# Layer 0's last image takes its norm, gate and projection band by band between its scans; layer 1's weights get another address

## The chip, the cores and the metric

The kernel runs on one core of a Trainium2 chip. A core has five engines that work side by side, each with its own instruction queue, executed in order: PE (TensorE, matrix products), DVE (VectorE), ACT (ScalarE), POOL (GpSimd) and SP, which here only issues transfers (DMAs). An instruction may wait on semaphores for work of other engines or for a transfer to land; everything queued behind it on its engine then waits too. The metric is device microseconds (us) of one execution; several runs are made and their median is given. Lines of the form L256 are line numbers of the kernel before.

## What is computed

The program is a stack of four layers on an input of 4 images, each 64x64 pixels of 128 channels; each layer adds its result to its input. The change lies in layer 0 and, for an address, in layer 1. Layer 0 is a two-dimensional selective scan (state space model) with 256 inner channels and 16 states:

```python
xz = x @ in_proj_w.T                      # x is group-normalized
xh, z = jnp.split(xz, 2, axis=-1)
z = silu(z)
xc = silu(depthwise_conv3x3(xh) + conv_b)
xs = stack([x0, x1, x0[..., ::-1], x1[..., ::-1]], axis=1)   # rows, columns, and both reversed
...
dA = jnp.exp(dt[..., None] * A)
h = dA * h + (dt * ut)[..., None] * bt[:, :, None, :]
y = jnp.einsum('bkdn,bkn->bkd', h, ct)
...
y = ys[:, 0] + ys[:, 2, :, ::-1]          # the four directions are added up (columns transposed)
...
mu = y.mean(-1, keepdims=True)
var = y.var(-1, keepdims=True)
y = (y - mu) / jnp.sqrt(var + EPS) * out_norm_w + out_norm_b
y = y * z
return y @ out_proj_w.T
```

The last five lines, per pixel over the 256 channels, are what the change moves for the last image: the norm, the gate `y * z` and the projection. Layers 1 (Fourier filters and a feed-forward part), 2 (a Fourier attention) and 3 (neighbourhood attention) follow.

## The kernel before

**Units and slots.** Layer 0 (`layer0`) works on one image after another. An image has 4096 pixels, cut into 8 bands (`NCH`) of 512 (`CH`). The scan of one band in one of the four directions is a *unit*: 32 units per image, 128 in all, directions in the order k = 1, 3, 0, 2, eight bands each. Directions 2 and 3 go through the bands backwards, so in the last eight units of an image (k = 2) band 7 comes first and band 0 last. Within a unit there are 16 *slots*, one per state (`NS`). A slot has one POOL product `dB` (L476), two ACT exponentials `dA` into PSUM (L482, three buffers), two DVE scans (L483), and a step of `transposed()`: PE transposes a piece of the states `h` of seven slots ago (`LAG`), ACT copies it out as `hT` (L380), PE multiplies it with C into `yT` (L405). At the unit's end DVE adds `yT` to `y` (L421); for k = 2, when all four directions are in, it also takes statistics of `y` (`bn_stats`, L424), and SP stores `y` to the scratch tensor `y2` (L426). Because of the lag this falls on slot 7 of the next unit; behind the very last scan the lag is worked off alone (`while queue or copied`).

**Order.** `manual_schedule` makes PE, ACT, DVE and POOL execute in the order in which the program calls them. SP's order is left to the framework's scheduler.

**Side work.** What is not a scan goes in between as generators, `before(b + 1)` (norm, gate and convolution inputs of the next image) and `after(b)` (what follows the scans of image b). A generator yields a letter for what its next piece needs: "l" loads, "f" is free to go anywhere, "m" needs the spare PSUM bank and so does not go into slots 6 to 10 (`BUSY`). A `Side` object paces it: `count` pieces over `slots` slots from slot `first`; a piece is due when its share of the time has passed. `later(place, ...)` puts a single instruction into a place of a coming slot.

**after(b).** First the statistics of all 32 pixel groups: 32 `bn_aggr` on DVE (L242) in four pieces, one square root on ACT and one reciprocal on DVE (`Shared.rstd`, L46 and L47), and a load of the table set for exponential and logarithm (`exp_and_ln`, L121), since the square root stands in another set. Then for each band: SP loads `yf` (from `y2`, L249) and `zf` (L251); DVE normalizes four 128x256 pieces (L256, two per "f" piece); PE transposes them into `pg` (L264) and ACT copies them out as `yg` with scale and bias (shown under L437, the line of the caller); POOL multiplies `yg` with the gate (L270) while SP loads the input `xr` (L269); PE projects (`op`, L275); DVE adds `xr` (L281, in `residual`) and SP stores the result to `x1` (L282). `after(b)` runs among the scans of image b + 1. For the last image there is no next one: `d.finish` runs it to its end behind the last scan.

**Layer 1 and 2.** Pools of SBUF memory are stacked in the order in which they are opened; a pool that is opened later takes the addresses of pools closed before. `layer1` opens its weights' pool `l1w` first, then its work pools, then loads the weights (`layer1_weights`, L581 on SP, L583 to L593 on ACT) and runs `layer1_image` four times: `load_image` (L701) and, at the end of each band, a store to `x2` (L696). Layer 2 then loads its own weights (L723).

Of the kernel before, what the change touches and what calls it, by code (L numbers as in the profile page):

```python
# [10 lines left out]
F32 = mybir.dt.float32  # L11
AF = mybir.ActivationFunctionType
ALU = mybir.AluOpType
AX = mybir.AxisListType
PSUM = bass.MemoryType.PSUM

P = 128
Q = 68
NB = 4
NT = 4096  # L20
DM = 128
NJ = NT // P
CH = 512
NCH = NT // CH
K4 = 4
WD = 32 * 129 * 16
NS = 16


class Shared:  # L30


    def __init__(self, tc, pool, A):
        nc = tc.nc
        self.nc, self.tc = nc, tc
        self.ident = pool.tile([P, P], F32, name="ident")
        make_identity(nc, self.ident)
        self.gmat = pool.tile([P, P], F32, name="gmat")
        nc.sync.dma_start(self.gmat, A["c_gmat"])
        self.eps5 = pool.tile([P, 1], F32, name="eps5")  # L40
        nc.vector.memset(self.eps5, 1e-5)
# [41 lines left out]
def layer0(sh, A, x_in, x_out, scr):  # L83
# [6 lines left out]
    tc, nc = sh.tc, sh.nc  # L90
    with ExitStack() as ctx:
        pool = lambda name, bufs, **kw: ctx.enter_context(tc.tile_pool(name=name, bufs=bufs, **kw))
        wp = pool("l0w", 1)
        tmp = pool("l0tmp", 2)
        small = pool("l0small", 2)
# [25 lines left out]
        exp_and_ln = lambda: nc.scalar.preload_act_table_set("natural_log_exp_and_others")  # L121
# [111 lines left out]
            nc.scalar.copy(xw, xo.rearrange("p (h w) -> p w h", w=64))  # L233
            nc.sync.dma_start(dst.rearrange("p (w h) -> p w h", h=64)[:, :, 8 * c : 8 * c + 8], xw)

        def after(b, st, later):

            mv = small.tile([P, NJ, 2], F32, name="ln_mv")
            for j in range(NJ):
                if j % 8 == 0:  # L240
                    yield "f"
                nc.vector.bn_aggr(mv[:, j, :], st[:, j])  # L242
            rs = sh.rstd(small, mv[:, :, 1], [P, NJ], "ln_r")
            exp_and_ln()
            for c in range(NCH):
                yield "l"
                rows = slice(c * CH, (c + 1) * CH)
                y = tmp.tile([P, 4, 2 * P], F32, name="yf", tag="t4", bufs=4)
                nc.sync.dma_start(y, tiles(scr(f"y2{b % 2}")[rows, :]))  # L249
                z = tmp.tile([P, 2, CH], F32, name="zf", tag="t4", bufs=4)  # L250
                nc.sync.dma_start(z, scr(f"z{b % 3}")[:, :, rows].rearrange("s p t -> p s t"))  # L251
                for q in range(4):
                    if q % 2 == 0:
                        yield "f"
                    j = 4 * c + q
                    nc.vector.tensor_scalar(  # L256
                        y[:, q, :], y[:, q, :], mv[:, j, 0:1], rs[:, j : j + 1], ALU.subtract, ALU.mult
                    )
                yg = tmp.tile([P, 2, CH], F32, name="yg", bufs=1)
                for s in range(2):  # L260
                    yield "m"
                    pt = spare("pg")
                    for q in range(4):
                        nc.tensor.transpose(pt[:, q * P : (q + 1) * P], y[:, q, s * P : (s + 1) * P], sh.ident)  # L264
                    norm = dict(scale=on_w[:, s : s + 1], bias=on_b[:, s : s + 1])
                    later("act0", nc.scalar.activation, yg[:, s, :], pt, AF.Identity, **norm)
                yield "f"
                xr = tmp.tile([P, 4, DM], F32, name="xr", tag="t2", bufs=4)
                nc.sync.dma_start(xr, tiles(x_in(b)[rows, :]))  # L269
                nc.gpsimd.tensor_tensor(yg, yg, z, ALU.mult)  # L270
                yield "m"
                op = spare("op").rearrange("p (q d) -> p q d", q=4)
                for q in range(4):
                    for s in range(2):
                        nc.tensor.matmul(  # L275
                            op[:, q, :], lhsT=yg[:, s, q * P : (q + 1) * P], rhs=w_out[:, s, :], start=(s == 0), stop=(s == 1)
                        )
                later("dve", residual, b, rows, xr, op)
# [65 lines left out]
        per = len(units) // NB  # L344
# [84 lines left out]
        sides = []  # L429
# [3 lines left out]
        slot = 0  # L433

        def later(place, f, *a, slots=1, **kw):

            todo.setdefault((slot + slots, place), []).append(lambda: f(*a, **kw))  # L437
# [10 lines left out]
        with tc.manual_schedule(engines=order):  # L448
            for i, (b, k, c) in enumerate(units):
                if i % per == 0:  # L450
                    ln_st = small.tile([P, NJ, 1, 6], F32, name="ln_st")
# [12 lines left out]
                for n in range(NS):  # L464
                    slot = NS * i + n
                    g, q = divmod(n, 4)
# [46 lines left out]
                    if n == 10:  # L513
                        y = unit["y"] = tmp.tile([P, 4, 2 * P], F32, name="y", tag="t4", bufs=4)
# [19 lines left out]
                    sides = [d for d in sides if d.need]  # L534
                if i + 1 < len(units):
                    u, bd, Wd = u_next, bd_next, Wd_next
                if i % per == per - 1:
                    slot += 1
                    for d in sides:
                        d.finish(flush_all)  # L540
                    sides = [Side(after(b, ln_st, later), 4 + 8 * 7, NS * (i + 1) + 8, 28 * NS)]
            while queue or copied:
                transposed()()
            for d in sides:
# [3 lines left out]
class Side:  # L548


    def __init__(self, pieces, count, first, slots):
        self.pieces, self.count, self.first, self.slots = pieces, count, first, slots
        self.done, self.run, self.free_at = 0, 0, first
        self.need = next(pieces)

# [3 lines left out]
        return self.need == "c" and self.run % 9 > 0  # L559

    def due(self, slot):
        return slot >= self.free_at and self.done * self.slots <= (slot - self.first) * self.count

    def step(self):
        self.done += 1
        self.run = self.run + 1 if self.need == "c" else 0
        self.need = next(self.pieces, None)
# [138 lines left out]
def layer1(sh, A, x_in, x_out):  # L706
    tc, nc = sh.tc, sh.nc
    with ExitStack() as ctx:
        pool = lambda name, bufs, **kw: ctx.enter_context(tc.tile_pool(name=name, bufs=bufs, **kw))
        wp = pool("l1w", 1)  # L710
        pools = pool("l1big", 2), pool("l1tmp", 2), pool("l1small", 2), pool("l1ps", 4, space=PSUM)
        w = layer1_weights(sh, A, wp)
        for b in range(NB):
            layer1_image(sh, w, pools, x_in(b), x_out(b))
# [1069 lines left out]
```

## Time and profile before

| What | us |
|---|---|
| median of 5 runs (8636.91 to 8653.36) | 8638.89 |
| the profiled execution, its own time | 8637.81 |
| its span, first to last instruction | 8636.0 |
| scans of image 0 (from 251.6) | 1456.1 |
| scans of image 1 | 1509.1 |
| scans of image 2 | 1509.0 |
| scans of image 3 (to 6132.8) | 1407.0 |
| behind the last scan, to the last residual of layer 0 | 115.1 |
| first load of layer 1's weights issued at | 6250.26 |
| first loads of layer 2 issued at | 6838.70 |

In the profile lines below, a group reads: line, engine, operation, output <- inputs, shapes, count | busy us, mean ns of one | idle us of the engine just before them, and what ended most of it. In an order of time a line reads: start us, duration us, engine, line, operation, tiles, shapes, count, and in brackets the engine's idle time before it and what released it. SPq and ACTq lines are the issue of a transfer, not its duration.

### The profile page before, as it was taken

To read this page: it belongs to the slowest core of one execution; us is meant where nothing else is said; L and a number is where in the kernel's file an instruction comes from. 1 tells how busy PE (TensorE), PEld (TensorE's weight loads), DVE (VectorE), ACT (ScalarE), POOL (GpSimd) and SP (SyncE) were. 2 spreads that over 40 slices of the span, in tenths; PEclk is the share of its full clock that TensorE was granted. 3 is DMA by queue.
4 is the path that set the end of the run, shared out by engine and by line. 5 is a ranking of instruction groups with operands and counts; after the bars stand their busy time and mean duration, and the time that the engine had idled before them with its cause. 6 is when DMAs were issued, how large, how long until landed. Compare 5 with 4: busy or idle time off the path is not lost. (4 is left out here: it accounts for less than half of the span.)

```text
span 8636.0 us, 140834 instructions
## 1 busy us (share of the span) xinstructions
PE 6675.1 (77%) x52976; PEld 4226.7 (49%) x52976; DVE 6815.9 (79%) x7900; ACT 6419.1 (74%) x10524; POOL 5539.1 (64%) x2518
## 2 busy tenths in 40 slices
PE   7688888777788777778877777777589677677689
PEld 3344454444445444444544444444377565464456
DVE  2689999998999999899999999999545533544578
ACT  6799999988888898888889989899422114416467
POOL 0689889988888898888889989999400010110233
PEclk9799999999999999999999999999789888788699
DMA  6345555445555454555545444445331231240332
GB/s 110 134 154 171 170 167 168 163 154 162 167 158 180 157 170 152 163 167 159 180 156 173 150 162 169 163 168 175 117 74 38 55 103 55 83 138 25 89 94 79
DMA packets 1292220, 1181.63 MB, mean 137 GB/s; under 512 B 640022, under 2 KB 1077874, under 8 KB 1224595
## 3 DMA queue, kind: packets, MB, share of 16 engines
q1 hardware_dynamic: 1289858, 1170.90, 43.4%
q8 instruction: 417, 6.83, 0.3%
q14 instruction: 265, 2.16, 0.1%
q10 hardware_dynamic: 1680, 1.74, 0.1%
HBM read 980.48 MB, written 189.74 MB: 136 GB/s over the span
## 5 line engine op out<-in xcount | busy, mean ns | idle before, releaser
L476 POOL TENSOR_TENSOR dB<-du,Bb 128x1024 f32<-128x1024 f32 x2048 | 4820.4, 2385 | 672.2 <-DVE h L483 496.6
L483 DVE TENSOR_TENSOR_SCAN h<-dA,state,dB 128x512 f32<-128x512 f32 x4096 | 4956.2, 1270 | 368.2 <-ACT dA L482 268.3
L370 PE MATMUL pt<-ident,h 128*128 128x128 f32 x16384 | 2267.1, 283 | 1070.6 <-ACT hT L380 1064.3
L482 ACT ACTIVATE dA<-delta,A_neg 128x512 f32<-128x512 f32 x4096 | 2748.1, 691 | 208.9 <-DVE h L483 185.9
L370 PEld LDWEIGHTS pt<-ident,h 128*128 128x128 f32 x16384 | 1853.7, 143 | 2119.8 <-ACT hT L380 1864.1
L380 ACT COPY hT<-pt 128x1024 f32<-128x1024 f32 x2048 | 2069.5, 1011 | 195.0 <-PE pt L370 180.1
L405 PE MATMUL yT<-hT,W 128*32 128x256 f32 x16384 | 1403.7, 415 | 3.1 <-DVE y L421 2.6
L206 PE MATMUL cv<-xn,taps 128*128 128x512 f32 x1152 | 620.0, 639 | 17.2 <-DVE e L222 8.7
L405 PEld LDWEIGHTS yT<-hT,W 128*32 128x32 f32 x16384 | 454.3, 150 | 355.6 <-issue 340.3
L857 POOL TENSOR_TENSOR xg<-xg,so 128x1024 f32<-128x1024 f32 x8 | 26.6, 3342 | 691.7 <-ACT so L857 670.7
L1506 POOL TENSOR_TENSOR S<-S,sm 128x784 f32<-128x784 f32 x128 | 191.1, 1493 | 407.5 <-DVE sm L1504 346.4
L316 PE MATMUL dp<-xd,w_dt 65*128 65x512 f32 x512 | 297.2, 663 | 128.0 <-ACT Ct L303 91.0
L325 POOL TENSOR_TENSOR du<-delta,u 128x1024 f32<-128x1024 f32 x128 | 304.9, 2382 | 81.7 <-DVE delta L322 81.7
L857 POOL TENSOR_TENSOR z<-z,sp 128x1024 f32<-128x1024 f32 x16 | 41.8, 2614 | 472.6 <-ACT z L857 472.3
L206 PEld LDWEIGHTS cv<-xn,taps 128*128 128x128 f32 x1152 | 185.1, 190 | 257.1 <-issue 241.6
L297 PE MATMUL xd_ps<-u,w_x 128*48 128x512 f32 x512 | 253.4, 619 | 48.2 <-DMA u<-l_xw 20.5
L1513 ACT ACTIVATE S<-S,mx 128x196 f32<-128x196 f32 x512 | 227.9, 448 | 34.6 <-DVE mx L1540 34.0
L857 PE MATMUL pz<-PT,WX 128*68 128x64 f32 x2048 | 164.0, 245 | 94.8 <-DVE WX L857 77.1
L857 POOL TENSOR_TENSOR WX<-wr,Xs 128x544 f32<-128x544 f32 x32 | 46.1, 1440 | 268.8 <-DMA wr<-wt 242.6
L857 PEld LDWEIGHTS pz<-PT,WX 128*68 128x68 f32 x2048 | 154.0, 159 | 119.0 <-DVE WX L857 77.0
L316 PEld LDWEIGHTS dp<-xd,w_dt 65*128 65x128 f32 x512 | 78.8, 194 | 242.8 <-ACT Ct L303 149.6
L672 ACT ACTIVATE h<-pf,b 128x512 f32<-128x512 f32 x128 | 88.0, 687 | 146.7 <-PE pf L671 146.7
(334 smaller groups left out, 7660.9 us busy)
## 6 DMA issues: line engine op xcount, KB each, us to landing
Bb<-l_B SPq DMA_DIRECT2D x512, 1024.0 KB
W<-l_W SPq DMA_DIRECT2D x512, 256.0 KB
l_y<-y SPq DMA_DIRECT2D x128, 512.0 KB
wr<-wt SPq DMA_DIRECT2D x256, 136.0 KB
u<-l_xw SPq DMA_DIRECT2D x64, 512.0 KB
y<-l_y SPq DMA_DIRECT2D x64, 512.0 KB
u<-l_xr SPq DMA_DIRECT2D x64, 512.0 KB
V<-l_v SPq DMA_DIRECT2D x512, 49.0 KB
```

The costliest lines, as they stand in the source:

```text
L206: nc.tensor.matmul(pm, lhsT=taps[:, s, t, :], rhs=xn[:, dy : dy + 8, dx : dx + 64], start=(t == 0), stop=(t == 8),)
L297: nc.tensor.matmul(xd_ps, lhsT=w_x[:, s, k, :], rhs=u[:, s, :], start=(s == 0), stop=(s == 1))
L316: nc.tensor.matmul(dp, lhsT=w_dt[:, k, s * P : (s + 1) * P], rhs=xd, start=True, stop=True)
L325: nc.gpsimd.tensor_tensor(du, delta, u, ALU.mult)
L370: nc.tensor.transpose(pt[:, j, s, :], G["h"][:, s, t0 : t0 + 32, :].rearrange("p t n -> p (t n)"), sh.ident)
L380: return lambda: nc.scalar.copy(hT, pt.rearrange("p j s d -> p j (s d)"))
L405: nc.tensor.matmul(U["yT"][e][32 * jo : 32 * jo + 32, qo % 2, :], lhsT=U["Ws"][G["g"]][:, :, 4 * q + j], rhs=hT[:, j, :], start=((e, jo) n ...
L476: nc.gpsimd.tensor_tensor(dB, du, B_now[:, q : q + 1, :].to_broadcast([P, 2, CH]), ALU.mult)
L482: nc.scalar.activation(dA, delta[:, s, :], AF.Exp, scale=A_neg[:, k, s, n : n + 1])
L483: nc.vector.tensor_tensor_scan(h[:, s, :, q], dA, dB[:, s, :], state[:, s, n : n + 1], ALU.mult, ALU.add)
L857: r = f(*args, **kw)
L1513: nc.scalar.activation(Sn, Sn, AF.Exp, bias=U["mx"][:, n : n + 1], accum_out=sm[:, n : n + 1])
```

## The change

The generator `after` takes the bands that it is to work on, and the statistics move into the band: four `bn_aggr`, then the reciprocal square root as exp(-0.5 ln(var + eps)), two ACT instructions on 128x4 from the table set that the scans use, directly behind the band's loads in the same piece "l". So Sqrt, reciprocal and the two table loads are gone for every image. `yg` has two buffers instead of one.

Images 0 to 2 run `after` as before, all bands in order, with 8·7 pieces instead of 4 + 8·7; image 2's is paced over 22 units instead of 28. For the last image a `Side` is added after the first of its last eight units, with the bands from 7 down to 0. Its list `loads` holds the slot from which each band's loads may go: slot 8 of the unit after the one that scanned the band. Apart from that its pieces are always due (`slots` is 1). What is left of it behind the last scan is run to the end there, after the lag is worked off.

In layer 1 the work pools are opened ahead of the weights' pool.

```diff
-        def after(b, st, later):
-
-            mv = small.tile([P, NJ, 2], F32, name="ln_mv")
-            for j in range(NJ):
-                if j % 8 == 0:
-                    yield "f"
-                nc.vector.bn_aggr(mv[:, j, :], st[:, j])
-            rs = sh.rstd(small, mv[:, :, 1], [P, NJ], "ln_r")
-            exp_and_ln()
-            for c in range(NCH):
+        def after(b, st, later, bands):
+
+            for c in bands:
                 yield "l"
...
+                mv = small.tile([P, 4, 2], F32, name="ln_mv")
+                for q in range(4):
+                    nc.vector.bn_aggr(mv[:, q, :], st[:, 4 * c + q])
+
+                rs = small.tile([P, 4], F32, name="ln_r")
+                nc.scalar.activation(rs, mv[:, :, 1], AF.Ln, bias=sh.eps5)
+                nc.scalar.activation(rs, rs, AF.Exp, scale=-0.5)
                 for q in range(4):
                     if q % 2 == 0:
                         yield "f"
-                    j = 4 * c + q
                     nc.vector.tensor_scalar(
-                        y[:, q, :], y[:, q, :], mv[:, j, 0:1], rs[:, j : j + 1], ALU.subtract, ALU.mult
+                        y[:, q, :], y[:, q, :], mv[:, q, 0:1], rs[:, q : q + 1], ALU.subtract, ALU.mult
                     )
-                yg = tmp.tile([P, 2, CH], F32, name="yg", bufs=1)
+                yg = tmp.tile([P, 2, CH], F32, name="yg", bufs=2)
...
-                    for d in sides:
-                        d.finish(flush_all)
-                    sides = [Side(after(b, ln_st, later), 4 + 8 * 7, NS * (i + 1) + 8, 28 * NS)]
+                    if b + 1 < NB:
+                        for d in sides:
+                            d.finish(flush_all)
+                    if b + 1 < NB:
+                        sides = [Side(after(b, ln_st, later, range(NCH)), 8 * 7, NS * (i + 1) + 8, (28 if b + 2 < NB else 22) * NS)]
+                elif b == NB - 1 and i % per == 3 * per // 4:
+
+                    done = [NS * (i + 1 + n) + 8 for n in range(NCH)]
+                    sides.append(Side(after(b, ln_st, later, range(NCH - 1, -1, -1)), 8 * 7, done[0], 1, done))
...
-    def __init__(self, pieces, count, first, slots):
-        self.pieces, self.count, self.first, self.slots = pieces, count, first, slots
+    def __init__(self, pieces, count, first, slots, loads=()):
+        self.pieces, self.count, self.first, self.slots, self.loads = pieces, count, first, slots, list(loads)
...
     def due(self, slot):
-        return slot >= self.free_at and self.done * self.slots <= (slot - self.first) * self.count
+        wait = self.need == "l" and self.loads and slot < self.loads[0]
+        return not wait and slot >= self.free_at and self.done * self.slots <= (slot - self.first) * self.count
 
     def step(self):
+        if self.need == "l" and self.loads:
+            self.loads.pop(0)
         self.done += 1
...
+        pools = pool("l1big", 2), pool("l1tmp", 2), pool("l1small", 2), pool("l1ps", 4, space=PSUM)
         wp = pool("l1w", 1)
-        pools = pool("l1big", 2), pool("l1tmp", 2), pool("l1small", 2), pool("l1ps", 4, space=PSUM)
```

## The prediction

> **What bounds the kernel now.** I read, in this order: the page's groups, the busy times by image, the order of time around the end of layer 0, and the order of time around single pieces of the work that moves.
>
> ```profile
> L476 POOL TENSOR_TENSOR dB<-du,Bb 128x1024 f32<-128x1024 f32 x2048 | 4820.4, 2385 | 672.2 <-DVE h L483 496.6
> L483 DVE TENSOR_TENSOR_SCAN h<-dA,state,dB 128x512 f32<-128x512 f32 x4096 | 4956.2, 1270 | 368.2 <-ACT dA L482 268.3
> ```
>
> Each of the 128 units makes 32 scans; VectorE scans, GpSimd supplies `dB`, ScalarE `dA`. They are nearly balanced, so a wait on one soon reaches the others. By stretch (from:to, length, busy us and instructions of PE, PEld, DVE, ACT and POOL, granted clock, DMA share, GB/s): image 2, image 3, and the tail behind the last scan:
>
> ```profile
> 3216.80:4725.80 1509.00, 1197.13 (x9174) 704.68 (x9170) 1400.41 (x1304) 1340.68 (x1991) 1298.92 (x567) 0.98 0.51 164
> 4725.80:6132.80 1407.00, 1047.80 (x8764) 639.25 (x8760) 1356.56 (x1240) 1266.37 (x1868) 1290.35 (x553) 0.97 0.46 161
> 6132.80:6247.90 115.10, 60.10 (x304) 44.89 (x296) 21.35 (x79) 22.17 (x26) 18.70 (x8) 0.63 0.32 103
> ```
>
> The last image's window has VectorE busy 96%; the 115 us behind it leave every engine mostly idle. That tail is what the change attacks:
>
> ```profile
> 6148.59 0.75 DVE L424 BATCH_NORM_STATS2 ln_st<-y 128x6 f32<-128x256 f32 x2
> 6149.26 2.27 DVE L242 BATCH_NORM_AGGREGATE ln_mv<-ln_st 128x2 f32<-128x6 f32 x32
> 6151.66 0.36 SPq L249 DMA_DIRECT2D yf<-l_y  x1
> 6155.56 1.38 DVE L256 TENSOR_SCALAR yf<-yf,ln_mv,ln_r 128x256 f32<-128x256 f32 x4 [3.29 <-DMA yf<-l_y]
> ...
> 6166.56 0.69 DVE L281 TENSOR_TENSOR xr<-xr,op 128x512 f32<-128x512 f32 x1 [9.62 <-PE op L275]
> ```
>
> The first band runs from 6155.56 to 6167.25: 11.7 us, a serial chain of DVE, PE, ACT, POOL, PE, DVE. The eighth band's residual ends at 6247.84, so the eight take 92.3 us, 11.5 each.
>
> **The change, part by part.**
>
> *1. Bands 7 to 1 leave the tail.* Read off the built order: with 32 units per image, units 25 to 31 of the last image each take one band's load, statistics and normalization; each residual comes in the next unit. Band 1's out_proj and band 0 stay behind the last scan. Band 1's out_proj follows the last yT (PE ends 6147.8) with the first band's 3.8 us and a 0.69 residual: 6152.3. SP stores it, 0.4, and only then issues band 0's `yf`: 6152.7, where before it was 6151.66. So band 0 ends 1.0 late, near 6168.3, and the tail loses 6247.84 - 6168.3 = **-79.5**. The shared statistics and the Sqrt that go from there cost nothing: the `yf` landing at 6155.5 covers them.
>
> *2. What a band costs between scans.* Its four 128x256 tensor_scalars take 1.38 in the tail, but not here:
>
> ```profile
> 5294.07 2.37 POOL L325 TENSOR_TENSOR du<-delta,u 128x1024 f32<-128x1024 f32 x1
> 5294.46 4.50 DVE L256 TENSOR_SCALAR yf<-yf,ln_mv,ln_r 128x256 f32<-128x256 f32 x2
> ...
> 5296.40 2.40 POOL L476 TENSOR_TENSOR dB<-du,Bb 128x1024 f32<-128x1024 f32 x1
> 5298.88 3.62 DVE L483 TENSOR_TENSOR_SCAN h<-dA,state,dB 128x512 f32<-128x512 f32 x3
> ```
> ```profile
> 5890.48 2.79 DVE L256 TENSOR_SCALAR yf<-yf,ln_mv,ln_r 128x256 f32<-128x256 f32 x2
> ```
>
> The first of a pair ends only when POOL's running operation does, the second waits for POOL's next: 4.50; where POOL has just ended, 2.79. The new places are after slots 11 and 12 of a unit, the first while `du` runs (as at 5294), the second after a scan slot. I take 4.50 + 2.79 = 7.29; bounds 5.6 (two fast pairs) and 9.0 (two slow).
>
> This is where a rule speaks against the change. The Trainium skill, SBUF — State Buffer, section Who interferes with whom, says VectorE in a two-port mode and GpSimd take the shared port pair for a whole instruction and the loser blocks fully, tensor_scalar being such an operation. Were each of the four blocked for a whole 2.38 us POOL operation, a band would cost about 11 us instead of 7.29, and the sum below would be 26 higher (an estimate); the rows show one of each fast pair not blocked.
>
> *3. The new wait.* The band's four bn_aggr (0.31, half of the 0.62 for eight below) are now followed by Ln and Exp on ACT, which stand in ACT's queue ahead of the next slot's `dA`. Before, ACT could run ahead. The Sqrt of the earlier image shows what such a wait does:
>
> ```profile
> 4810.44 0.62 DVE L242 BATCH_NORM_AGGREGATE ln_mv<-ln_st 128x2 f32<-128x6 f32 x8
> 4811.09 0.32 ACT L46 ACTIVATE ln_r<-ln_mv,eps 128x32 f32<-128x32 f32 x1 [0.79 <-DVE ln_mv L242]
> 4811.43 1.28 ACT L121 ACT_TABLE_LOAD   x1
> 4812.73 1.30 ACT L482 ACTIVATE dA<-delta,A_neg 128x512 f32<-128x512 f32 x2
> 4813.51 4.81 DVE L483 TENSOR_TENSOR_SCAN h<-dA,state,dB 128x512 f32<-128x512 f32 x4 [1.71 <-ACT dA L482]
> ```
>
> ACT starts when bn_aggr is done, and the next scan starts 0.78 after `dA` does: the scans stood 4813.51 - 4811.06 = 2.45. With Ln and Exp on 128x4 (0.29 each, by the row of that size in layer 1, no loads between) it is 0.03 + 0.29 + 0.02 + 0.29 + 0.02 + 0.78 = **1.42 per band**. At slot 9 a delta operation of 0.66 fills part of it, but ACT then lacks the lead for its extra Exp and Ln at slot 10, so I keep 1.42. Lower bound 0.58, ACT's own work alone; queued behind it are `dA`, hence every scan, and the `hT` copy, hence PE.
>
> *4. POOL, PE and ACT's copies.* POOL's `yg` product (2.34) now comes one slot after ACT's second copy, so POOL waits there and its lead in `dB` shrinks. Over the last image's scans VectorE waited 12.2 us for `dB` in 12 places, 1.5 for each of eight bands, but only 1.0 in all in its last quarter; I take 1.0 a band (bounds 0 and 1.83). Residual 0.66. PE's transposes and out_proj are hidden: PE is busy 31 of 41.5 us in a clean unit; uncovered, out_proj would add its 3.8. ACT's two copies (0.78 each in the tail) lie beside the `yf` pairs, in which ACT waits for VectorE; uncovered, 1.6 a band.
>
> Seven bands pay 7.29 + 0.31 + 1.42 = 9.02, **+63.1**; six pay 1.66 in the next unit, **+10.0**. So the last image gains only 79.5 - 73.1 = 6.4, because a band costs nearly as much among the scans as in the tail. A whole band of the image before, over units 25 to 28, cost 8.4 without bn_aggr, Ln and Exp (174.6 against four clean units of 41.55), which agrees with 7.29 + 0.66.
>
> *5. The other three images' bands use the same new code.* 24 bands × 1.42 = **+34.1**; three Sqrt waits of 2.45 go, **-7.4**; bn_aggr is as many as before. Image 2's bands in 22 instead of 28 units only shift places: 0 (±5 by the two pair prices). Bounds of the new wait here too: 0.58 and 1.42.
>
> The Trainium skill, ScalarE: Activation LUTs, section Table sets, gives about 5.3 us for the two loads that exp-then-sqrt costs. By that figure the saving would be three times 2.8 larger, 8 us off the sum (an estimate); this trace's loads take 1.28 each.
>
> *6. SP.* In units 25 to 31 `yf` waits for the landing of the `y` store issued just before it (3.08 us from issue to release at 6148.58 to 6151.66). Queued behind it are `zf`, the next `y` and the next unit's first `Bb`. Four DMAs a band come into these units (`yf`, `zf`, `xr`, the `x1` store, some 0.4 of SP each); SP's own issue time is small beside a 41.5 us unit. That `Bb` was issued 5.2 us after the store in the unit at 6030 (6030.60 against 6035.77), so the wait is covered: 0; uncovered, 3.08 a unit.
>
> *7. The weights' home.* In the built order the `w1` load still stands last in SP and waits for the last `x1` store, so layer 1 starts as before: 0. Layer 2's first loads, issued at 6838.70 ahead of the last `x2` store (6839.62), now wait for it to land: 6839.62 + 3.08 is 4.0 later; later lane waits shrink, so bounds 0 and +4, taken **+2.0**.
>
> Sum: -79.5 + 63.1 + 10.0 + 34.1 - 7.4 + 2.0 = **+22.3**. The profiled execution took 8637.81 (span 8636.0 and 1.8 around it), 1.1 below the median of five: 8660.
>
> **The rivals.**
> *ACT's wait is hidden* (the other side). Place: after each bn_aggr; price: 31 × 1.42 = 44.0. For it: ACT idles some 2.3 us in a clean unit, and VectorE's waits for POOL in the yf pairs give ACT time. Against: 4813.51. Fully hidden: 22.3 - 44.0, **8616**. The sign turns where a wait costs less than 1.42 - 22.3 / 31 = 0.70.
> *The balance.* Half of that wait is taken back in the slots behind: 22.3 - 22 = +0.3, **8638**, no change. For it: ACT's slack above; in the first eight units of an image ACT stalls VectorE anyway, so that new waits partly replace old ones.
> *SP late.* The store lands later under traffic and `Bb` is late in seven units: 7 × 3.08, **8682**. Against: the 5.2 us of cover. For: DMA is half busy there.
> *The weights come early* and spare layer 1's wait (6250.26 to 6258.67, 8.4 us): **8652**. Against: `w1`'s place in SP.
>
> **How the numbers follow.** Forecast 0.48, its own range 8646 to 8676; hidden 0.12; balance 0.25; SP late 0.12; early weights 0.03. What a measurement here can tell from no change is 0.2%, 17 us. Faster 0.12 (hidden), same 0.28 (balance, early weights), slower 0.60 (forecast, SP late). All lower bounds together give 8614, all upper ones 8679, with SP late above it; leaving out most of hidden, the range is 8622 to 8688.
>
> **What would show it.** Right: the last image's units 25 to 31 at 50 to 52 us instead of 41.5; the tail after the last scan near 36 us; gaps of about 1.4 us before scans released by ACT after each bn_aggr, in all of images 1 to 3; images 1 and 2 some 9 us longer each. Wrong: yf pairs near 1.4 us; no ACT gap; scans waiting for `Bb`; units 25 to 31 below 48.

## The result and the profile after

| | us |
|---|---|
| before, median of 41 runs (8630.58 to 8664.42) | 8641.07 |
| after, median of 21 runs (8647.47 to 8679.67) | 8661.8 |
| after / before, 95% interval | 1.0024 (1.0018 to 1.0030) |
| profiled execution after (before) | 8666.40 (8637.81) |
| its span | 8664.6 (8636.0) |

The changed kernel is slower by a quarter of a per cent, some 21 us. The two profiled executions lie 28.6 apart, 8 more than the medians, so a stage carries some of the spread of single executions; the table cuts the 28.6 into stages (a unit or an image runs from its first scan to the next one's first scan; most lines of the changed kernel carry numbers one below those of before). In the column of predictions, the 8.4 us of the band of image 2 that lay in units 25 to 28 stand with units 0 to 24, where the tighter pacing puts it.

| stage | before | after | difference | predicted |
|---|---|---|---|---|
| up to the first scan | 251.7 | 254.6 | +2.9 | 0 |
| image 0 | 1456.1 | 1456.1 | 0.0 | 0 |
| image 1 | 1509.2 | 1512.4 | +3.2 | +8.9 |
| image 2 | 1509.0 | 1514.2 | +5.2 | +8.9 |
| image 3, units 0 to 24 | 1108.7 | 1127.1 | +18.4 | +17.3 |
| image 3, units 25 to 31 | 298.1 | 369.1 | +70.9 | +64.7 |
| last scan to last residual | 115.1 | 36.3 | -78.8 | -79.5 |
| from there to layer 1's first statistics | 21.6 | 21.4 | -0.2 | 0 |
| from there to the end | 2366.6 | 2373.4 | +6.9 | +2.0 |

The page's groups of the changed kernel, the two lines that answer to those of before:

```profile
L482 DVE TENSOR_TENSOR_SCAN h<-dA,state,dB 128x512 f32<-128x512 f32 x4096 | 4962.7, 1270 | 415.8 <-ACT dA L481 309.2
L475 POOL TENSOR_TENSOR dB<-du,Bb 128x1024 f32<-128x1024 f32 x2048 | 4819.2, 2384 | 730.8 <-DVE h L482 495.9
```

The work is the same to a few us (scans 4962.7 busy against 4956.2). What has grown is the idle time before scans, from 368.2 to 415.8, and 40.9 of those 47.6 us were ended by ScalarE's `dA`. The same three stretches as before, image 2, image 3, tail:

```profile
3223.10:4737.20 1514.10, 1213.02 (x9170) 715.04 (x9170) 1397.37 (x1303) 1340.61 (x2004) 1297.70 (x567) 0.97 0.51 164
4737.20:6233.50 1496.30, 1096.00 (x8897) 669.79 (x8896) 1406.71 (x1301) 1278.79 (x1908) 1306.97 (x561) 0.95 0.46 158
6233.50:6269.80 36.30, 20.81 (x160) 14.58 (x160) 5.93 (x16) 9.15 (x12) 2.82 (x2) 0.81 0.15 51
```

The tail shrank as planned, but image 3 is 89 us longer while VectorE's busy time in it rose by only 50: the rest is waiting. The tail in order of time:

```profile
6250.06 0.69 DVE L420 TENSOR_TENSOR y<-y,yT 128x512 f32<-128x512 f32 x1 [2.00 <-PE yT L404]
6250.78 0.36 SPq L425 DMA_DIRECT2D l_y<-y  x1
...
6252.01 0.69 DVE L280 TENSOR_TENSOR xr<-xr,op 128x512 f32<-128x512 f32 x1 [0.47 <-PE op L274]
...
6253.60 0.36 SPq L242 DMA_DIRECT2D yf<-l_y  x1
...
6258.03 1.39 DVE L255 TENSOR_SCALAR yf<-yf,ln_mv,ln_r 128x256 f32<-128x256 f32 x4 [5.05 <-DMA yf<-l_y]
...
6269.10 0.69 DVE L280 TENSOR_TENSOR xr<-xr,op 128x512 f32<-128x512 f32 x1 [9.68 <-PE op L274]
```

Band 1's residual starts 2.0 us after the last sum of `y`; only band 0 follows, with its chain of 11.8 us. Next, where a moved band pays. First the directly visible wait, from unit 29 of the last image:

```profile
6102.29 0.35 DVE L247 BATCH_NORM_AGGREGATE ln_mv<-ln_st 128x2 f32<-128x6 f32 x4
...
6102.56 0.65 DVE L321 SCALAR_TENSOR_TENSOR delta<-delta,dp 128x512 f32<-128x512 f32 x1
6102.68 0.30 ACT L250 ACTIVATE ln_r<-ln_mv,eps 128x4 f32<-128x4 f32 x1 [1.80 <-DVE ln_mv L247]
...
6103.01 0.20 ACT L251 ACTIVATE ln_r<-ln_r 128x4 f32<-128x4 f32 x1
6103.12 1.28 ACT L481 ACTIVATE dA<-delta,A_neg 128x512 f32<-128x512 f32 x2
...
6103.89 3.63 DVE L482 TENSOR_TENSOR_SCAN h<-dA,state,dB 128x512 f32<-128x512 f32 x3 [0.68 <-ACT dA L481]
...
6107.72 1.29 DVE L482 TENSOR_TENSOR_SCAN h<-dA,state,dB 128x512 f32<-128x512 f32 x1 [0.19 <-ACT dA L481]
```

ScalarE, which used to run ahead, stands 1.80 us before Ln until the last `bn_aggr` is done; `dA` stands behind it, so the scan does too: 1.33 us from 6102.56 to 6103.89, of which a delta operation fills half and 0.68 stays open. Such a gap follows every one of the 31 groups of `bn_aggr` among the scans: 1.25 us in 19 places where a scan comes next, 0.87 (0.68 and 0.19, as above) in ten where a delta operation comes first, and 0.75 in two behind a piece of the next image's norm; 34 us together, 1.1 each. In 28 of them `dA` came last, in three GpSimd's `dB`. A little later in the same band (the second half of `yf`, the gate product and the scans after it):

```profile
6118.98 2.43 DVE L255 TENSOR_SCALAR yf<-yf,ln_mv,ln_r 128x256 f32<-128x256 f32 x1
...
6125.76 0.78 ACT L436 ACTIVATE yg<-pg,cols 128x512 f32<-128x512 f32 x1 [0.41 <-PE pg L263]
...
6126.61 2.38 POOL L269 TENSOR_TENSOR yg<-yg,zf 128x1024 f32<-128x1024 f32 x1 [5.35 <-ACT yg L436]
...
6128.95 25.78 POOL L475 TENSOR_TENSOR dB<-du,Bb 128x1024 f32<-128x1024 f32 x11
...
6131.34 2.46 DVE L482 TENSOR_TENSOR_SCAN h<-dA,state,dB 128x512 f32<-128x512 f32 x2 [2.87 <-POOL dB L475]
```

GpSimd had the `dB` of the coming slots to make, but the gate product stands in front in its queue and waits 5.35 us for ScalarE's second copy. Then it runs 2.38, and the lead in `dB` is gone: VectorE waits 2.87.

### The profile page after: what moved, and what is told of

It reads as the page before. It is cut to its first block, busy times and chain, and to the rows that moved or that the text cites. A ratio compares the mean times of both kernels' runs of the same rounds, so it can differ in the third digit from the quotient of the medians.

```text
span 8664.6 us, 140873 instructions
## 1 busy us (share of the span) xinstructions
PE 6716.6 (78%) x52976; PEld 4251.1 (49%) x52976; DVE 6848.1 (79%) x7896; ACT 6418.2 (74%) x10576; POOL 5536.1 (64%) x2518
## 5 line engine op out<-in xcount | busy, mean ns | idle before, releaser
L482 DVE TENSOR_TENSOR_SCAN h<-dA,state,dB 128x512 f32<-128x512 f32 x4096 | 4962.7, 1270 | 415.8 <-ACT dA L481 309.2
L369 PE MATMUL pt<-ident,h 128*128 128x128 f32 x16384 | 2293.4, 285 | 1062.1 <-ACT hT L379 1055.8
L369 PEld LDWEIGHTS pt<-ident,h 128*128 128x128 f32 x16384 | 1879.0, 145 | 2111.2 <-ACT hT L379 1855.8
L865 POOL TENSOR_TENSOR xg<-xg,so 128x1024 f32<-128x1024 f32 x8 | 26.6, 3339 | 696.5 <-DMA xg<-x 646.8
```

The costliest lines, as they stand in the source:

```text
L369: nc.tensor.transpose(pt[:, j, s, :], G["h"][:, s, t0 : t0 + 32, :].rearrange("p t n -> p (t n)"), sh.ident)
L482: nc.vector.tensor_tensor_scan(h[:, s, :, q], dA, dB[:, s, :], state[:, s, n : n + 1], ALU.mult, ALU.add)
L865: r = f(*args, **kw)
```

## The experiments

Each run was compared with the kernel before on the same chip (4 to 11 executions of the run, 7 to 25 of before). Differences to the changed kernel are differences of these ratios times 8641 us.

| run | median | ratio to before (95%) |
|---|---|---|
| weights' old home | 8663.8 | 1.0023 (1.0013 to 1.0032) |
| shared Sqrt for images 0 to 2 | 8638.8 | 0.9988 (0.9979 to 0.9997) |
| yg two slots later | 8650.9 | 1.0010 (1.0000 to 1.0020) |
| yf by scalar_tensor_tensor | 8676.7 | 1.0038 (1.0025 to 1.0050) |
| Ln and Exp one slot later | 8619.3 | 0.9975 (0.9966 to 0.9983) |
| yf in the accumulator form | 8572.8 | 0.9922 (0.9909 to 0.9934) |
| yf on ScalarE | 8567.2 | 0.9906 (0.9893 to 0.9920) |
| three edits together (3, 5 and 6) | 8523.7 | 0.9860 (0.9837 to 0.9883) |
| before, with accumulator form | 8556.7 | 0.9898 (0.9878 to 0.9918) |
| three edits, half of yf on ScalarE | 8502.4 | 0.9830 (0.9812 to 0.9849) |
| three edits, last image back in the tail | 8581.1 | 0.9922 (0.9909 to 0.9935) |
| edits 3 and 5 alone | 8611.7 | 0.9958 (0.9946 to 0.9971) |

**1. The weights' home**

```diff
-        pools = pool("l1big", 2), pool("l1tmp", 2), pool("l1small", 2), pool("l1ps", 4, space=PSUM)
         wp = pool("l1w", 1)
+        pools = pool("l1big", 2), pool("l1tmp", 2), pool("l1small", 2), pool("l1ps", 4, space=PSUM)
```

> The changed kernel with the second layer's weights back in their old place in SBUF; nothing else differs. Theory (the weights' home costs little: layer 2's first loads wait for the last x2 store): 2 us less than the changed kernel's 8661.8, so 8660, which a timing can't tell from it, but in the trace layer 2's first load of its constants (an) comes ahead of the last x2 store again, and the stretch from layer 1's first gn_st to that load is 569 us as before instead of the changed kernel's 574. Rival (the new home spares layer 1 a wait): the gap from the last residual of layer 0 to layer 1's first gn_st, 21.4 in the changed kernel, grows by several us. Rival (the home is what made layers 1 to 3 together 6.9 us longer): 8655.

The time doesn't tell it from the changed kernel, as expected. In the trace the stretch from layer 1's first `gn_st` to layer 2's first load is 566.9 us; with the old home it is 569.2 (before) and 569.1 (the run of before with the accumulator form), with the new one 570.9 to 574.0 in all the others. So the new home costs about 4.5 us of waiting there. Layer 1 is not spared anything: the gap ahead of it is 21.8 here, 21.4 after. From `gn_st` to the end, executions spread from 2363 to 2377 whatever the home, so that the 6.9 of the table can't be put down to the change, and no run shows the 4.5 us in the time.

**2. The statistics of images 0 to 2 shared again**

```diff
+            shared = b + 1 < NB
+            if shared:
+                mv = small.tile([P, NJ, 2], F32, name="ln_mv_all")
+                for j in range(NJ):
...
+                    nc.vector.bn_aggr(mv[:, j, :], st[:, j])
+                rs = sh.rstd(small, mv[:, :, 1], [P, NJ], "ln_r_all")
+                exp_and_ln()
...
-                        sides = [Side(after(b, ln_st, later, range(NCH)), 8 * 7, NS * (i + 1) + 8, (28 if b + 2 < NB else 22) * NS)]
+                        sides = [Side(after(b, ln_st, later, range(NCH)), 4 + 8 * 7, NS * (i + 1) + 8, (28 if b + 2 < NB else 22) * NS)]
```

> Images 0 to 2 take their statistics up front with one Sqrt again; the last image keeps its bands, Ln and Exp. Theory (each band's bn_aggr followed by Ln and Exp makes the scans wait for dA): images 1 and 2 go back to 1509 us each (from 1512.4 and 1514.2), the last image's units 0 to 24 lose some 9 of their 1127; in all -17: 8645, ratio 1.0004. As predicted at 1.42 a band it would be -27: 8635. Rival (Ln and Exp are hidden, and the last image's longer window comes from packing image 2's bands into 22 units): the last image's units 0 to 24 stay at 1127 and the sum is within 5 us of the changed kernel, 8657 to 8662.

The kernel gains 0.36%, 31 us (the predicted price of 24 bands less three Sqrt waits was 27). Image 1 is 1508.1, image 2 1511.8, and units 0 to 24 of the last image 1107.1 (from 1127.1), while units 25 to 31 stay at 368.5. The rival, that packing image 2's bands into 22 units made them dear, falls: the packing is still there. By stage the price of 27 does not come out, though: images 1 and 2 lose 6.7 us where it says 17.8, units 0 to 24 of the last image 20.0 where it says 8.9. The run also goes back to 4 + 8·7 pieces and so to the old places of the pieces, so that its 31 us are not the price of the wait alone; experiment 5 takes the wait out without that.

**3. The gate product two slots later**

```diff
+                if b == NB - 1:
+                    yield "f"
+                    yield "f"
                 yield "f"
                 xr = tmp.tile([P, 4, DM], F32, name="xr", tag="t2", bufs=4)
```

> In the last image alone, GpSimd's yg product is issued two slots later. Theory (GpSimd stands 5.4 us in front of each yg waiting for ScalarE's second copy, uses up its lead in dB, and VectorE then waits 2.8 us for dB in each of units 25 to 30): the 5.4 goes, the 2.8 falls below 0.5, units 25 to 30 go from 53.5 to some 51, in all -14 to -17: 8646. Rival (it is GpSimd's own 2.38 us that is too much for a unit in which it has 16 dB, du and yg to do): the wait only moves to a later scan, units stay at 53 to 53.5, 8660.

Units 26 to 30 go to 51.4 to 51.8, units 25 to 31 together from 369.1 to 357.5, -11.6; the time falls by 0.14%, 12 us. That is a little less than expected: VectorE's waits for `dB` over these units go from 16.9 to 2.2, but the residual now waits for PE, 0.43 in each of six units. The waits of GpSimd over units 25 to 31, after and here (us in total, times, longest):

```profile
POOL yg L269 <- ACT yg L436: 37.2, 7, 5.4
POOL dB L475 <- DVE h L482: 21.0, 14, 2.7
```

```profile
POOL dB L478 <- issue: 27.2, 13, 2.7
POOL dB L478 <- DVE h L485: 25.2, 20, 2.7
...
POOL yg L272 <- ACT yg L439: 5.4, 1, 5.4
```

Of 37.2 us before `yg` only the last unit's 5.4 are left, since there the product still has to wait. What GpSimd idles otherwise lies before `dB`, and where a scan ends it (25.2), it has filled its three buffers: that is a lead, and idle time before `yg` used it up. The first window holds no wait for `Bb`, which the rival "SP late" needed.

**4. yf by scalar_tensor_tensor**

```diff
-                    nc.vector.tensor_scalar(
-                        y[:, q, :], y[:, q, :], mv[:, q, 0:1], rs[:, q : q + 1], ALU.subtract, ALU.mult
-                    )
+                    scale = rs[:, q : q + 1].to_broadcast([P, 2 * P])
+                    nc.vector.scalar_tensor_tensor(y[:, q, :], y[:, q, :], mv[:, q, 0:1], scale, ALU.subtract, ALU.mult)
```

> yf's normalization by scalar_tensor_tensor (the scale as a broadcast operand) in place of tensor_scalar, in all bands; same arithmetic. Theory (the 6.2 to 7.4 us of a band's four tensor_scalars are waiting for GpSimd's running operation; the work itself is 0.35 each): the four take about 1.4 to 1.6 among the scans too; the 28 bands of the images' windows lose (192 - 124 x 0.37 = 146 us), the one in the tail nothing: 8661.8 - 146 = 8516, ratio 0.985; units 25 to 30 near 47.5. Rival (the time is VectorE's own, or scalar_tensor_tensor is held up in the same way): no change, 8660. Rival (what VectorE no longer loses in yf it loses waiting for dB and dA, since GpSimd and ScalarE have no more slack): half of it, 8590.

A miss: no gain but 0.14%, 12 us, more. All 128 instances by duration (ns, min/median/max), after and here:

```profile
L255 DVE TENSOR_SCALAR yf<-yf,ln_mv,ln_r x128: 379/2149/2466, 1757.7 to 6259.0; 128x256 f32<-128x256 f32 x128
```

```profile
L256 DVE SCALAR_TENSOR_TENSOR yf<-yf,ln_mv,ln_r x128: 448/2278/2593, 1756.1 to 6266.1; 128x256 f32<-128x256 f32 x128
```

Alone it takes 448 ns, but among GpSimd's products it is held just as long. Units 26 to 29 of the last image are 54.0. So it is not tensor_scalar as such that is held. Nor is it scalar_tensor_tensor as such: the delta operation of every unit is one, on twice the elements, with one tensor in SBUF and one in PSUM, and none of its 256 instances in the changed kernel is held:

```profile
L321 DVE SCALAR_TENSOR_TENSOR delta<-delta,dp x256: 652/661/689, 243.6 to 6162.5; 128x512 f32<-128x512 f32 x128
```

**5. Ln and Exp one slot later**

```diff
-                nc.scalar.activation(rs, mv[:, :, 1], AF.Ln, bias=sh.eps5)
-                nc.scalar.activation(rs, rs, AF.Exp, scale=-0.5)
+                later("act1", nc.scalar.activation, rs, mv[:, :, 1], AF.Ln, bias=sh.eps5)
+                later("act1", nc.scalar.activation, rs, rs, AF.Exp, scale=-0.5)
```

> In all bands Ln and Exp are issued one slot after the four bn_aggr, behind that slot's dA in ScalarE's queue; the arithmetic is the same. Theory (the price of the per-band statistics is ScalarE standing before Ln until bn_aggr is done, with dA queued behind): the gap of 0.87 us before a scan in units 25 to 30 goes, and with 24 earlier bands at about 1 us each the whole is -20 to -25 (what the shared Sqrt brought): 8638. Rival (the price is ScalarE's own 0.6 us for Ln and Exp in a queue that has no slack): the gap shows up one slot later, and the time stays within 6 us of 8662.

The gain is 0.49%, 42 us, twice what was expected and enough to make the kernel faster than before. The place of the wait, unit 29 of this kernel:

```profile
6058.63 0.35 DVE L247 BATCH_NORM_AGGREGATE ln_mv<-ln_st 128x2 f32<-128x6 f32 x4
6058.90 0.66 DVE L321 SCALAR_TENSOR_TENSOR delta<-delta,dp 128x512 f32<-128x512 f32 x1
6059.47 4.80 DVE L482 TENSOR_TENSOR_SCAN h<-dA,state,dB 128x512 f32<-128x512 f32 x4
```

No gap before the scan, nor before a later one: ScalarE's own 0.5 us is hidden, the standing before Ln was the price. The gap directly behind `bn_aggr` is gone in all 31 places. VectorE's waits over images 1 and 2 show it in bulk (before, after, this run):

```profile
DVE h L483 <- ACT dA L482: 134.9, 220, 1.7
DVE h L483 <- POOL dB L476: 55.4, 26, 2.9
DVE h L483 <- issue: 5.2, 6, 1.3
```

```profile
DVE h L482 <- ACT dA L481: 161.5, 237, 1.9
DVE h L482 <- POOL dB L475: 42.4, 24, 2.9
```

```profile
DVE h L482 <- ACT dA L481: 135.0, 219, 1.9
DVE h L482 <- POOL dB L475: 43.0, 22, 2.9
```

The changed kernel waits 26.6 us longer for `dA` in these 16 bands, 1.66 each (18.3 of it directly behind `bn_aggr`), and this edit takes all of it away. It also shows why images 1 and 2 grew by 8.4 only: the waits for `dB` fell by 13.0 and those of unknown end by 5.0 at the same time, and `yf` took 90.0 us there instead of 98.9. The second buffer of `yg` did not do this: the run of experiment 2 has it too, with the old 60 pieces, and stands where the kernel before does, with 98.9 us in `yf` and these waits:

```profile
DVE h L493 <- ACT dA L492: 133.6, 218, 1.9
DVE h L493 <- POOL dB L486: 55.8, 27, 2.9
DVE h L493 <- issue: 6.6, 9, 1.3
```

What is left is where the pieces fall: 56 over 28 units instead of 60, the `bn_aggr` inside the bands.

**6. yf in the accumulator form.** Two tensor_scalars, each also writing out an accumulator that nothing reads:

```diff
+                dump = small.tile([P, 2], F32, name="dump")
...
                     nc.vector.tensor_scalar(
-                        y[:, q, :], y[:, q, :], mv[:, q, 0:1], rs[:, q : q + 1], ALU.subtract, ALU.mult
+                        y[:, q, :], y[:, q, :], mv[:, q, 0:1], None, ALU.subtract, ALU.add, accum_out=dump[:, 0:1]
+                    )
+                    nc.vector.tensor_scalar(
+                        y[:, q, :], y[:, q, :], rs[:, q : q + 1], None, ALU.mult, ALU.add, accum_out=dump[:, 1:2]
                     )
```

> Each of yf's tensor_scalars becomes two, one subtracting the mean and one multiplying by the scale, both in the form that also writes out its accumulator (to a scratch column that nothing reads): one SBUF tensor in, no second element a cycle. Theory (what holds VectorE is any instruction that reads SBUF over two ports, one tensor at double rate or, as the scalar_tensor_tensor run showed, two tensors; reads over one port, like bn_stats at 0.42, are free of GpSimd): eight instructions of some 0.4 us and their accumulator reads, 3.3 to 4 us a band instead of 6.2 to 7.4: 28 bands x 3 = -85, 8575, ratio 0.9925, and units 25 to 30 near 50. Rival (any write of VectorE to SBUF of that size waits for GpSimd): eight waits instead of four, +150 or more: above 8800.

As expected: -1.02%, 88 us. Twice the instructions, none of them held (ns, min/median/max):

```profile
L256 DVE TENSOR_SCALAR_CACHE_REDUCE yf<-yf,ln_mv x128: 448/474/480, 1758.4 to 6176.9; 128x256 f32<-128x256 f32 x128
L256 DVE DVE_READ_ACCUMULATOR yf<-yf,ln_mv x128: 76/83/89, 1758.7 to 6177.3; 128x1 f32 x128
```

From the start of each pair to the next scan, a band's `yf` in units 25 to 30 takes twice 1.82 us of VectorE's time, 3.6, instead of 7.1. The Trainium skill, SBUF — State Buffer, section Who interferes with whom, has both this run and the miss above: it lets VectorE contend with GpSimd through tensor_scalar but "not the form that also writes out its accumulator", and also through any instruction with two SBUF inputs, which the scalar_tensor_tensor of experiment 4 had and its expectation overlooked. The medians, 474 against 2149 and 2278 ns, and the 661 of the delta operation, agree with it. The ports themselves are in no trace; what the runs show is which forms are held.

**7. yf on ScalarE**

```diff
+                mr = small.tile([P, 4], F32, name="ln_mr")
+                later("dve", nc.vector.scalar_tensor_tensor, mr, mv[:, :, 0], -1.0, rs, ALU.mult, ALU.mult)
...
-                    nc.vector.tensor_scalar(
-                        y[:, q, :], y[:, q, :], mv[:, q, 0:1], rs[:, q : q + 1], ALU.subtract, ALU.mult
-                    )
+                    nc.scalar.activation(y[:, q, :], y[:, q, :], AF.Identity, scale=rs[:, q : q + 1], bias=mr[:, q : q + 1])
```

> yf's normalization moves to ScalarE: Identity with scale 1/sigma and bias -mean/sigma, which VectorE works out in one small scalar_tensor_tensor (128x4). Theory (ScalarE reads SBUF without waiting for GpSimd, but has only some 2.3 us of slack in a clean unit): VectorE loses 6.2 to 7.4 us of held time a band and gains 0.2; ScalarE gains four activations of about 0.45, on the path where its slack is used up: 28 bands x (6.9 - 0.2 - 1.8) = -137, 8525, ratio 0.9865, units 25 to 30 near 47.5. Rival (ScalarE is the second bound everywhere, and the activations stand in front of dA as Ln and Exp do): each band gives back 4 us or more, 8600.

-1.18%, 102 us: between the two expectations (8525 and 8600). Units 25 to 30 are 49.5 to 50.9. One reason is a small instruction that was priced at 0.2:

```profile
L257 ACT ACTIVATE yf<-yf,ln_mr,ln_r x128: 585/596/615, 1754.0 to 6165.0; 128x256 f32<-128x256 f32 x128
L436 DVE SCALAR_TENSOR_TENSOR ln_mr<-ln_mv,ln_r x32: 163/1636/2907, 1732.6 to 6159.5; 128x4 f32<-128x4 f32 x32
```

ScalarE's pieces are never held, though they take 0.6 us each where the expectation had 0.45. VectorE's four elements per partition, with two SBUF inputs, are: 0.16 us alone, 1.6 in the median.

**8 to 10. Three edits together; before with the cheap yf; half of yf on ScalarE.** The first joins edits 3, 5 and 6. The second puts edit 6 into the kernel before, for images 0 to 2 only. The third starts from the first and gives two of a band's four pieces to ScalarE:

```diff
+                nc.vector.tensor_scalar(mr, mv[:, :, 0], -1.0, None, ALU.mult, ALU.add, accum_out=dump[:, 0:1])
...
+                for q in (2, 3):
+                    later("act1", nc.scalar.activation, mr[:, q : q + 1], mr[:, q : q + 1], AF.Identity, scale=rs[:, q : q + 1])
...
+                    if q < 2:
...
+                    else:
+                        norm = dict(scale=rs[:, q : q + 1], bias=mr[:, q : q + 1])
+                        nc.scalar.activation(y[:, q, :], y[:, q, :], AF.Identity, **norm)
```

> The changed kernel with three of the earlier edits together: yf's normalization in two tensor_scalars with accumulator, Ln and Exp one slot later, and the last image's yg two slots later. Theory (three separate prices: VectorE held in yf -89, ScalarE standing before Ln -42, GpSimd standing before yg -11, each as its own run showed against the changed kernel's 8661.8): they add up to -142, 8520, ratio 0.986; units 25 to 30 near 46.5 with no wait for dB above 0.5. Rival (the prices share one slack, so that what one edit frees another wait takes up): about half of the two smaller ones, 8545.

> The kernel before, with yf's normalization in two tensor_scalars with accumulator in the bands of images 0 to 2 (the last image's eight, in the tail, keep the old form). Theory (a band among scans costs 6.6 us in yf here and 4.4 in the new form, GpSimd being left alone): 24 x 2.2 = -53: 8588. The changed kernel with the same form took 8573, so that with bands that are not held the change comes out 15 us, 0.2%, ahead, where it lies 0.2% behind as written: the sign of the change hangs on what a band costs among the scans. Rival (yf's price is no part of the change's balance): this kernel gains as much as the changed one did, 89 us, 8552, and the change stays behind by 20.

> As the run with the three edits together, but two of a band's four 128x256 pieces are normalized on ScalarE (Identity with scale and bias, the bias made by a small accumulator tensor_scalar and two activations of 128x1). Theory (VectorE is the bound among the scans, and with Ln, Exp and yg out of the way ScalarE has the 1.4 us to spare): VectorE loses some 2.0 a band, half of it comes out: 31 x 1.0 = 31 below that run, 8490. Rival (ScalarE has nothing to spare, as its activations stand in front of dA): no better than that run, 8520 to 8530.

The three prices add up: 8523.7, 0.9860, expected 8520 and 0.986. Units 25 to 31 are 45.5 to 47.5; the longest wait for `dB` there is 0.7, where 0.5 was expected. The kernel before, though, gained 90 us from the cheap `yf` and not 53, as much as the changed one: the expectation priced a band at 4.4 from summed records that overlap, where it takes 3.6 (24 bands x (6.6 - 3.6) = 72), and 16 more went from the idle time before scans (368.2 to 352.3). So the rival stands: changed against before is 0.9922 / 0.9898 = 1.0024 with the cheap form (uncertain by as much again, by the two intervals) and 1.0024 without. To that accuracy the held `yf` is a cost of both kernels and not what decides the sign. Half on ScalarE brings 0.30%, 26 us, more (8502.4): the fastest kernel of the study, 0.9830 of before (0.9812 to 0.9849).

**11 and 12. What the move is worth, and the two waits alone**

```diff
-                    if b + 1 < NB:
-                        for d in sides:
-                            d.finish(flush_all)
-                    if b + 1 < NB:
-                        sides = [Side(after(b, ln_st, later, range(NCH)), 8 * 7, NS * (i + 1) + 8, (28 if b + 2 < NB else 22) * NS)]
-                elif b == NB - 1 and i % per == 3 * per // 4:
...
+                    for d in sides:
+                        d.finish(flush_all)
+                    sides = [Side(after(b, ln_st, later, range(NCH)), 8 * 7, NS * (i + 1) + 8, 28 * NS)]
```

> The run with the three edits together (8523.7), but the last image's eight bands go back behind its last scan, and image 2's bands take 28 units again; images 0 to 2 keep the bands' own statistics with Ln and Exp one slot later. It tells how much of that run's gain is the moving of the last image's bands. Theory (a moved band costs 4.8 us among the scans there, units 25 to 31 being 325.9 us long against 294.6 where none was moved, plus a few us for packing image 2 tighter): the tail grows by 78, the image loses 31 to 45: +33 to +47, 8557 to 8571. Rival (the gain is the bands' own statistics in images 0 to 2, which alone made images 1 and 2 shorter by 13 and 7 us where the wait was taken away): within 10 us of 8524. Against the kernel before with the same form of yf (8557) the theory has the statistics worth nothing, the rival has them worth all of 33.

> The changed kernel with yf's normalization as it stands, and only its two new waits taken out: Ln and Exp one slot later in all bands, yg two slots later in the last image's. Theory (the two waits are what turned the change from a gain into a loss): -42 and -11 add up against 8661.8: 8608, ratio 0.9965, faster than before, with the bands as dear in yf as before (7.4 us). Rival (the held yf alone makes the move not worth while, the earlier gain of the later Ln being a matter of where pieces fall): 8625 to 8645.

Without the moved bands the time rises by 0.62%, 54 us, more than expected. 24 of it is the accumulator form in the tail, which the expectation forgot: that tail is 137.8 long, and 113.7 with the old form, as nothing there holds VectorE. Of the rest, 30 us is the move; and 0.9922 less those 24 us (0.0028) is 0.9894, against 0.9898 for before with the cheap `yf`: within the intervals the bands' own statistics are worth nothing either way once Ln doesn't block. The last run is the changed kernel with Ln and Exp, and in the last image the gate product, put later and nothing else: 0.9958, 57 us below the changed kernel (expected 54) and 36 below before, with `yf` still held. VectorE's waits over its units 25 to 31, after and here:

```profile
DVE h L482 <- POOL dB L475: 16.9, 6, 2.9
DVE h L482 <- ACT dA L481: 6.9, 14, 1.3
```

```profile
DVE h L485 <- POOL dB L478: 3.0, 6, 0.7
DVE xr L283 <- PE op L277: 2.1, 5, 0.4
DVE h L485 <- ACT dA L484: 0.9, 1, 0.9
```

## Why the prediction was right, and where its sizes were off

The forecast was 8660 for 8661.8, or +22.3 us for +20.7, by its own mechanism: a tail emptied, and the emptied work nearly as dear among the scans, with a new wait on ScalarE in every band as what tips it. Taking that wait alone out (experiment 5) turns the sign, so the mechanism is shown. That sum and time agree to 2 us is luck: the terms below miss by -9.4, +6.2 and more, and cancel in part. Step by step:

1. *The tail*, -79.5: -78.8. Right, band 1 and band 0 included.
2. *The yf pairs*, 7.29 a band: 7.23 to 7.25 in units 25 to 30 with the overlap of the records counted once, and 5.50 in unit 31; 48.9 in all seven instead of 51.0. Right.
3. *The wait for Ln*, 1.42 a band, 44.0 in all 31: the gaps behind `bn_aggr` add up to 34, 1.1 each, as Exp took 0.20 instead of 0.29 and the delta operation, where it comes first, does fill part, as the prediction saw and then set aside. Taking the wait away brought 42, so some 8 us more hung on it elsewhere. Right in mechanism, and nearly in sum. In units 25 to 31 the edit gave 1.14 a band (369.1 to 361.1). The rival "hidden" needed the wait below 0.70. The rival "balance", half of it taken back, falls by the same 42.
4. *GpSimd's stall before yg*, 1.0 a band: 2.8. This term was mis-sized. The row it was taken from (`dB` waits of the old bands among scans) has pieces eight slots apart, where ScalarE's copy was long done when GpSimd came to `yg`; in the new order one slot lies between. VectorE waits 16.9 us for `dB` there, where the term stood for 6, and edit 3 gives 11.6 back. The 10.9 too few, less 2.0 for the smaller wait of step 3 (7 x 0.28) and 2.1 for step 2, are about the 6.2 us by which these units came out longer than predicted. So units 25 to 30 are 52.9 to 53.6 long, where the sign of being right was 50 to 52.
5. *Images 1 and 2*, +17.8: +8.4. The waits for `dA` rose by 26.6, 8.8 more than these 17.8; but 26.9 came off (13.0, 5.0 and 8.9, as under experiment 5) by the new places of the pieces, for which the prediction has no term in these images, and smaller items make up the rest. Other executions of the same code for these images gave +17.1 and +13.2 (the first and third experiments), so part is spread.
6. *The weights' home*, +2.0: about 4.5 of waiting in the trace, not visible in the time. *SP*, 0: no `dB` waited for `Bb` in units 25 to 31, as "SP late" needed. *Early weights*: layer 1's gap stayed, 21.6 and 21.4.
7. *The port.* The prediction weighed a rule on tensor_scalar's two ports; the price it took from rows was right, but what is held is wider (two SBUF inputs) and avoidable (accumulator form), and it belongs to both kernels.

That the change could have paid was in reach of the prediction's rival with the other sign: the kernel with Ln's wait alone out lies at 8619, near the 8616 of "hidden", and with both waits out at 8612. It needed two instructions, and the gate product, to be put later.

## What to carry to other kernels

When work moves from an idle tail into a balanced pipeline, price what it does to the lead of the engines that feed the pipeline: an instruction that waits on another engine blocks everything behind it in its queue, and put one or two slots later, when its operand is long done, it costs only itself. Take the price of a wait from a row with the same distance to its producer. On VectorE beside a busy GpSimd, count an instruction by its SBUF inputs and not by its elements, and look for a form that reads one tensor over one port.

## What the hardware showed that was not expected

- A VectorE instruction on 128x4 elements with two SBUF inputs took 163 ns at its fastest and 1636 in the median beside GpSimd's products of 2.4 us.
- Two accumulator-form tensor_scalars and their two accumulator reads are faster among the scans than the single tensor_scalar they replace (3.6 us against 7.1 for a band's four pieces in units 25 to 30), and slower where GpSimd has no `dB` to make (3.0 us more a band in the tail).
- The same code for images 1 and 2 took 1512.4, 1518.9 and 1516.6 us for image 1 in three executions, a spread as large as some of the terms above.
